# Layer 0 of a graph network: values split in two halves, second moments half a batch later in the order

## The chip, the cores and the metric

The kernel runs on one core of one Trainium2 chip. The metric is the device time of the whole program in microseconds (us). Engines are named TensorE (matmul; PE in the profile, with PEld for its weight loads), VectorE (DVE), ScalarE (ACT), GpSimd (POOL), and SyncE (SP), which issues loads.

## The reference

Sixteen graphs of 1024 nodes with 128 features go through four layers, each followed by a residual sum and a layer norm. Only layer 0 is touched here. Per graph, `adj` is a 0/1 matrix:

```python
w = masked_row_softmax(transpose(adj))      # row: region, column: node
region = matmul(w, features)
region = batch_norm(matmul(region, kernel_1) + bias_1, gamma_1, beta_1)
people = matmul(transpose(w), region)
people = batch_norm(matmul(people, kernel_2) + bias_2, gamma_2, beta_2)
x = layernorm(x + people)
```

Since the entries are 0 or 1, the softmax row is the mask divided by the number of its ones (the degree). Both batch norms take mean and variance over all graphs and nodes. Layers 1 to 3 are attention layers over the same graphs.

## The kernel before, in words

All arrays of a graph ("batch" b, 16 of them) are cut into C = 8 chunks of 128 rows. The kernel has two stages. The first, up to about 395 us, is class `Pass`: it reads `adj` once and computes for every batch mask-times-features, and then transposed-mask times that, without the small matrices. As batch norms are linear once their statistics are known, it gathers only the first and second moments of both results (`moments1`, `moments2`, each one PSUM bank that accumulates over all batches). Then a short serial part turns the moments into scales. The second stage (classes `Norm` and `Batch`) finishes layer 0 from the stored products `people` and runs layers 1 to 3.

One batch of the first stage has these steps:

- `load` (line 483) loads `x` and splits it into a high part in the matmul's short format (ScalarE, line 488) and a low remainder (VectorE, line 489), both in `x2`.
- `cast` (line 495), per chunk: load 512 KB of `adj` into `at`, and convert it into the mask `m`; even chunks on VectorE (line 501), odd ones on ScalarE (line 499). `at` has four buffers, `m` three.
- `forth` (line 503), per chunk: eight matmuls into `pz`; ScalarE copies the low half into `lo` (line 508), VectorE adds both into `z` (line 509). The mask's row sums, the degrees, come out as an extra column.
- `split` (line 511), once: reciprocal degrees `r` (lines 513 to 516), `reg` = `z` times `r` (line 520), `v` = `reg` times `r` (line 523), and `v` parted into a high part on ScalarE (line 525) and a low remainder on VectorE (line 526), both in `v2`. `reg` and `v` have one buffer each.
- `moment1` (line 531), per chunk: `reg` times itself into `moments1`, two matmuls in the profile.
- `back` (line 536), per chunk: eight matmuls of the mask with `v2` into `pb`; ScalarE copies the low half (line 543), VectorE adds (line 544) into `g`.
- `moment2` (line 546), per chunk: `g` times itself into `moments2`.
- `store` (line 551): one statistics instruction on `g` and the DMA of `g` to `people`. `g` has two buffers, `pz` and `pb` two PSUM banks each.

The order is written out with due times (lines 555 to 564). A step of batch b gets a time in units of batches; the per-chunk steps are spread over 0.9 of a unit; all are sorted and traced in that order. So in unit b the core runs `forth` of batch b beside `moment1`, `back` and `moment2` of batch b - 1, and casts of batch b + 1. The sorted order sets priorities: an instruction whose inputs or buffer aren't there yet (in the planner's own estimate) lets later ones past on its engine. On the chip each engine then follows its planned list.

Of the kernel before, what the change touches and what calls it, by code (L numbers as in the profile page):

```python
# [8 lines left out]
F32 = mybir.dt.float32  # L9
# [3 lines left out]
ALU = mybir.AluOpType  # L13
# [3 lines left out]
P = 128  # L17
# [10 lines left out]
F32R = mybir.dt.float32r  # L28
# [362 lines left out]
def fast_path(ctx, tc, x, adj, adjt, k1, k2, w1, vecs, b_w, b_a, out, bad):  # L391


    nc = tc.nc
    B, N, D = x.shape
    C = N // P
    H = N // 512
    G = C // 4
    A = D + 1
# [34 lines left out]
    degs = const.tile([P, B, C], F32, name="degs")  # L434
# [33 lines left out]
    with tc.tile_pool(name="z_load", bufs=4) as zl, tc.tile_pool(name="z_mask", bufs=3) as zm, \  # L468
# [8 lines left out]
        class Pass:  # L477
# [30 lines left out]
                nc.scalar.copy(self.lo[:, c, :], pz[:, D:D + A])  # L508
                nc.vector.tensor_tensor(self.z[:, c, :], pz[:, :D], self.lo[:, c, :D], ALU.add)  # L509

            def split(self):

                nc.vector.tensor_copy(degs[:, self.b, :], self.lo[:, :, D])
                r = zw.tile([P, C], F32, name="r")
                nc.vector.tensor_scalar(r, self.lo[:, :, D], 1.0, None, ALU.max)
                nc.vector.reciprocal(r, r)
                self.reg = zw.tile([P, C, A + 1], F32, name="reg", bufs=1)
                nc.gpsimd.memset(self.reg[:, :, D:], 1.0)
                by = r[:, :, None]
                nc.vector.tensor_tensor(self.reg[:, :, :D], self.z, by.to_broadcast([P, C, D]),  # L520
                                        ALU.mult)
                v = zw.tile([P, C, A], F32, name="v", bufs=1)
                nc.vector.tensor_tensor(v, self.reg[:, :, :A], by.to_broadcast([P, C, A]), ALU.mult)
                self.v2 = zw.tile([P, C, 2, A], F32R, name="v2")
                nc.scalar.copy(self.v2[:, :, 0, :], v)
                nc.vector.tensor_tensor(self.v2[:, :, 1, :], v, self.v2[:, :, 0, :].bitcast(F32),  # L526
                                        ALU.subtract)
                self.g = zw.tile([P, C, A + 1], F32, name="g")
                nc.gpsimd.memset(self.g[:, :, A:], 1.0)

            def moment1(self, c):
                nc.tensor.matmul(moments1[:, :A + 1], self.reg[:, c, :D], self.reg[:, c, :],  # L532
# [22 lines left out]
        order = []  # L555
        for b in range(B):
            s = Pass(b)
            for t, fs in ((b - 1, (s.load,)), (b + 0.95, (s.split,)), (b + 2.1, (s.store,))):
                order += [(t, f) for f in fs]
            for t, f in ((b - 0.95, s.cast), (b, s.forth), (b + 1, s.moment1), (b + 1.05, s.back),  # L560
                         (b + 1.2, s.moment2)):
                order += [(t + 0.9 * c / C, lambda f=f, c=c: f(c)) for c in range(C)]
        for _, f in sorted(order, key=lambda o: o[0]):
            f()
# [135 lines left out]
    with tc.tile_pool(name="r_load", bufs=3) as loads, tc.tile_pool(name="r_rows", bufs=2) as rows, \  # L700
# [220 lines left out]
        order = []  # L921
# [47 lines left out]
def kernel(tc, x, adj, adjt, k1, k2, w1, vecs, b_w, b_a, out):  # L969
    nc = tc.nc  # L970
    with tc.tile_pool(name="keep", bufs=1) as keep:
        bad = keep.tile([1, 1], I32, name="bad")
        fast_path(tc, x, adj, adjt, k1, k2, w1, vecs, b_w, b_a, out, bad)

        again = nc.values_load(bad[0:1, 0:1])
        with tc.If(again > 0):
            general_path(tc, x, adj, adjt, k1, k2, w1, vecs, b_w, b_a, out)
# [39 lines left out]
```

## Time and profile before

The time is 1988.63 us, the median of 3 runs (1984.18 to 1992.79). The profiled execution took 1994.7 us with a mean granted TensorE clock of 0.951.

| in the first stage | value |
|---|---|
| TensorE busy, whole span | 1742.4 us, 87% |
| VectorE busy, whole span | 1536.7 us, 77% |
| ScalarE busy, whole span | 997.1 us, 50% |
| line 506, `forth` matmuls | 1024 of 306 ns |
| line 539, `back` matmuls | 1024 of 295 ns |
| line 520 / 523 / 526, VectorE, 1024 to 1032 elements | 1.23 us each, 16 times |
| line 525, ScalarE, the high part of `v` | 1.06 us, 16 times |
| TensorE's wait at line 547 (`moment2`) for `g` | 25.6 us in 14 waits |
| TensorE's wait at line 539 (`back`) for the low part of `v` | 14.4 us in 14 waits |

How to read it: matmuls are pipelined, so a matmul's listed duration is longer than the distance to the next one (some 130 ns within a `forth` group); idle time between matmuls counts, not the sum of their durations. A wait is put down to the instruction that ended it last.

### The profile page before, as it was taken

How to read it: one execution, taken by the hardware profiler on the slowest of the kernel's cores; microseconds unless marked ns; L12 is line 12 of the kernel's file. 1: busy time of each engine (PE TensorE's matmuls, PEld its weight loads, DVE VectorE, ACT ScalarE, POOL GpSimd, SP SyncE). 2: the span in 40 equal slices, each digit the busy share in tenths (PEclk: the TensorE clock that was granted, in tenths of full speed). 3: DMA queues.
4: the chain of work that ended last, by engine and by line, in shares of the span. 5: the costliest groups of instructions: out<-in, count | busy, mean ns of one | idle time of the engine just before them, and what ended most of it. 6: DMA issues, size and time to landing. Idle time of an engine off the chain costs nothing.

```text
span 1994.7 us, 26348 instructions
## 1 busy us (share of the span) xinstructions
PE 1742.4 (87%) x9453; PEld 1260.5 (63%) x9453; DVE 1536.7 (77%) x3707; ACT 997.1 (50%) x1793; POOL 147.8 (7%) x252
## 2 busy tenths in 40 slices
PE   6988888957879999999999998998999999999895
PEld 6988888833545666656565655665665656565574
DVE  4554444467979789897989798989889898979765
ACT  4533334235455565545555556465565545555533
POOL 0000000001001010101000101101010101000100
PEclk9999899968999999999999999999999999999998
DMA  8866565143413232241404041323222240402000
GB/s 298 282 238 222 208 232 189 40 146 118 149 59 95 69 96 92 72 133 32 151 25 141 23 142 55 110 69 102 76 94 95 70 133 32 130 14 71 11 1 23
DMA packets 110958, 216.39 MB, mean 108 GB/s; under 512 B 7776, under 2 KB 63712, under 8 KB 110816
## 3 DMA queue, kind: packets, MB, share of 16 engines
q1 hardware_dynamic: 108512, 206.08, 31.6%
q10 hardware_dynamic: 2304, 8.52, 1.1%
q8 instruction: 76, 1.25, 0.3%
q14 instruction: 66, 0.54, 0.1%
HBM read 197.67 MB, written 16.91 MB: 108 GB/s over the span
## 4 chain that ended last, share of the span: by engine, by line
PE 42%; DVE 35%; ACT 8%; DMA 6%; POOL 4%; issue 4%; SPq 0%; DVEq 0%; ACTq 0%
PE pacc L876 17%; PE pbig L863 6%; DVE e L834 5%; PE pb L539 5%; PE po L844 5%; DVE e L837 5%; PE pz L506 5%; DMA at<-in_adj_dram 4%; ACT m L499 2%; DVE ln_st L718 2%; PE moments L547 1%; DVE e L831 1%; POOL rs_t L442 1%; PE pacc L753 1%; DVE hn L813 1%
## 5 line engine op out<-in xcount | busy, mean ns | idle before, releaser
L844 PE MATMUL po<-e,hn 128*128 128x512 f32 x512 | 251.8, 621 | 13.9 <-ACT hn L841 13.7
L823 ACT ACTIVATE pen<-adjt,minus_root 128x1024 fp8e5<-128x1024 int32 x128 | 146.5, 1148 | 74.9 <-DMA adjt<-in_adjt_dram 74.5
L844 PEld LDWEIGHTS po<-e,hn 128*128 128x128 f32 x512 | 94.6, 195 | 131.2 <-issue 82.0
L506 PE MATMUL pz<-x,m 128*128 128x258 f32 x1024 | 164.9, 306 | 4.6 <-ACT m L499 2.3
L539 PE MATMUL pb<-v,m 128*128 128x258 f32 x1024 | 151.2, 295 | 15.8 <-DVE v L526 14.4
L834 DVE SCALAR_TENSOR_TENSOR e<-u,q,u 128x1024 f32<-128x1024 f32 x128 | 161.4, 1271 | 0.3 <-ACT q L816 0.3
L837 DVE SCALAR_TENSOR_TENSOR e<-e,adjt 128x1024 f32<-128x1024 f32 x128 | 154.5, 1216 | 0.0
L539 PEld LDWEIGHTS pb<-v,m 128*128 128x128 f32 x1024 | 137.0, 198 | 18.7 <-DVE v L526 17.0
L506 PEld LDWEIGHTS pz<-x,m 128*128 128x128 f32 x1024 | 140.4, 202 | 7.3 <-ACT m L499 3.4
L880 DVE TENSOR_SCALAR sums<-pacc 128x3 f32<-128x3 f32 (+1 forms) x96 | 14.5, 151 | 145.9 <-PE pacc L876 145.9
L544 DVE TENSOR_TENSOR g<-pb,lo 128x129 f32<-128x129 f32 x128 | 36.4, 291 | 97.6 <-ACT lo L543 97.3
L841 ACT ACTIVATE hn<-hn,rs 128x128 f32<-128x128 f32 x128 | 49.9, 398 | 119.6 <-DVE rs L840 91.8
L831 DVE SCALAR_TENSOR_TENSOR e<-adjn,adjt 128x1024 f32<-128x1024 int32 (+7 forms) x128 | 95.2, 744 | 6.2 <-PE po L844 3.9
L499 ACT CAST m<-at 128x1024 fp32r<-128x1024 int32 x64 | 67.5, 1054 | 62.4 <-DMA at<-in_adj_dram 62.4
L509 DVE TENSOR_TENSOR z<-pz,lo 128x128 f32<-128x128 f32 x128 | 35.7, 288 | 76.4 <-ACT lo L508 76.2
L508 ACT COPY lo<-pz 128x129 f32<-128x129 f32 x128 | 34.1, 267 | 83.8 <-PE pz L506 83.0
L547 PE MATMUL moments<-g 128*128 128x130 f32 x256 | 53.1, 290 | 25.6 <-DVE g L544 25.6
L543 ACT COPY lo<-pb 128x129 f32<-128x129 f32 x128 | 33.0, 268 | 72.2 <-PE pb L539 72.1
L501 DVE CAST m<-at 128x1024 fp32r<-128x1024 int32 x64 | 43.8, 685 | 21.3 <-DMA at<-in_adj_dram 21.3
L547 PEld LDWEIGHTS moments<-g 128*128 128x128 f32 x256 | 41.6, 200 | 28.2 <-issue 27.2
L532 PE MATMUL moments<-reg 128*128 128x130 f32 x256 | 39.8, 279 | 2.8 <-DVE reg L520 2.1
L813 DVE TENSOR_TENSOR hn<-pacc,bw_row 128x387 f32<-128x387 f32 (+1 forms) x48 | 23.0, 502 | 21.3 <-PE pacc L811 21.0
(1169 smaller groups left out, 4239.1 us busy)
## 6 DMA issues: line engine op xcount, KB each, us to landing
at<-in_adj_dram SPq DMA_DIRECT2D x128, 512.0 KB, 5.3
adjt<-in_adjt_dram SPq DMA_DIRECT2D x128, 512.0 KB, 3.5
people<-g ACTq DMA_DIRECT2D x16, 520.0 KB, 5.9
g<-people SPq DMA_DIRECT2D x16, 520.0 KB, 4.6
xf<-in_x_dram SPq DMA_DIRECT2D x16, 512.0 KB, 6.3
adjn<-in_adj_dram SPq DMA_DIRECT2D x16, 512.0 KB, 4.4
x<-in_x_dram SPq DMA_DIRECT2D x16, 512.0 KB, 4.7
adjn<-in_adj_dram SPq DMA_DIRECT2D x16, 448.0 KB, 4.5
```

What stands on the lines that cost most here:

```text
L499: nc.scalar.copy(self.m[:, i, :], at)
L506: nc.tensor.matmul(pz[:, :2 * A], self.m[:, i, c * P:(c + 1) * P], self.x2[:, i, :], start=(i == 0), stop=(i == C - 1))
L539: nc.tensor.matmul(pz[:, :2 * A], self.m[:, j, c * P:(c + 1) * P], self.v2[:, j].rearrange("p s a -> p (s a)"), start=(j == 0), stop=(j == ...
L547: nc.tensor.matmul(moments2[:, :A + 1], self.g[:, c, :D], self.g[:, c, :], start=(self.b == 0 and c == 0), stop=(self.b == B - 1 and c == ...
L823: nc.scalar.activation(self.pen[:, c, :], at, AF.Square, bias=minus_root, scale=BIG_ROOT, saturate=False, accum_out=checks[:, self.b, c:c ...
L831: nc.vector.scalar_tensor_tensor(e[:, :n], an[:, :n], 1.0, at[:, c * P:], ALU.mult, ALU.not_equal, accum_out=unlike[:, self.b, c:c + 1])
L834: nc.vector.scalar_tensor_tensor(e, self.u2, self.q[:, c:c + 1], self.u1, ALU.mult, ALU.max)
L837: nc.vector.scalar_tensor_tensor(e, e, 1.0, at, ALU.mult, ALU.mult, accum_out=total)
L841: nc.scalar.mul(self.hn[:, c, :D], self.hn[:, c, :D], rs)
L844: nc.tensor.matmul(self.po[:, cols], self.hn[:, c, :D], e[:, cols], start=(c == 0), stop=(c == C - 1))
L863: nc.tensor.matmul(ps[:, cols], self.xw[:, c * P:(c + 1) * P], self.xt[:, cols], start=True, stop=True)
L876: nc.tensor.matmul(po[:, k, :], self.e[:, m, c * P:(c + 1) * P], xl[:, m, :], start=(m == 0), stop=(m == C - 1))
```

## The change

`split` becomes two calls, `split(0)` on chunks 0 to 3 and `split(1)` on chunks 4 to 7. The first also makes the tiles `reg`, `v2` and `g` and their constant columns. `r` and `v` are now half as large, and `v` has two buffers. The first half is due at b + 0.48, when half of `forth` has been traced, the second at b + 0.93 (the whole was at b + 0.95). In the order, `moment1` goes from b + 1 to b + 1.05, `back` from b + 1.05 to b + 1.12, `moment2` from b + 1.2 to b + 1.6, and `store` from b + 2.1 to b + 2.6. The purpose is that the values for `back` are prepared while `forth` is still running, and that the second moments aren't asked for right after the `back` that makes their `g`.

```diff
-            def split(self):
-                nc.vector.tensor_copy(degs[:, self.b, :], self.lo[:, :, D])
-                r = zw.tile([P, C], F32, name="r")
-                nc.vector.tensor_scalar(r, self.lo[:, :, D], 1.0, None, ALU.max)
+            def split(self, h):
+                if h == 0:
+                    self.reg = zw.tile([P, C, A + 1], F32, name="reg", bufs=1)
+                    nc.gpsimd.memset(self.reg[:, :, D:], 1.0)
+                    self.v2 = zw.tile([P, C, 2, A], F32R, name="v2")
+                    self.g = zw.tile([P, C, A + 1], F32, name="g")
+                    nc.gpsimd.memset(self.g[:, :, A:], 1.0)
+                n = C // 2
+                c = slice(h * n, (h + 1) * n)
+                nc.vector.tensor_copy(degs[:, self.b, c], self.lo[:, c, D])
+                r = zw.tile([P, n], F32, name="r")
+                nc.vector.tensor_scalar(r, self.lo[:, c, D], 1.0, None, ALU.max)
                 nc.vector.reciprocal(r, r)
...
-                nc.vector.tensor_tensor(self.reg[:, :, :D], self.z, by.to_broadcast([P, C, D]),
-                                        ALU.mult)
-                v = zw.tile([P, C, A], F32, name="v", bufs=1)
-                nc.vector.tensor_tensor(v, self.reg[:, :, :A], by.to_broadcast([P, C, A]), ALU.mult)
...
-                nc.scalar.copy(self.v2[:, :, 0, :], v)
-                nc.vector.tensor_tensor(self.v2[:, :, 1, :], v, self.v2[:, :, 0, :].bitcast(F32),
+                nc.vector.tensor_tensor(self.reg[:, c, :D], self.z[:, c, :],
+                                        by.to_broadcast([P, n, D]), ALU.mult)
+                v = zw.tile([P, n, A], F32, name="v", bufs=2)
+                nc.vector.tensor_tensor(v, self.reg[:, c, :A], by.to_broadcast([P, n, A]), ALU.mult)
+                nc.scalar.copy(self.v2[:, c, 0, :], v)
+                nc.vector.tensor_tensor(self.v2[:, c, 1, :], v, self.v2[:, c, 0, :].bitcast(F32),
                                         ALU.subtract)
...
-            for t, fs in ((b - 1, (s.load,)), (b + 0.95, (s.split,)), (b + 2.1, (s.store,))):
-                order += [(t, f) for f in fs]
-            for t, f in ((b - 0.95, s.cast), (b, s.forth), (b + 1, s.moment1), (b + 1.05, s.back),
-                         (b + 1.2, s.moment2)):
+            order += [(b - 1, s.load), (b + 0.48, lambda s=s: s.split(0)),
+                      (b + 0.93, lambda s=s: s.split(1)), (b + 2.6, s.store)]
+            for t, f in ((b - 0.95, s.cast), (b, s.forth), (b + 1.05, s.moment1),
+                         (b + 1.12, s.back), (b + 1.6, s.moment2)):
                 order += [(t + 0.9 * c / C, lambda f=f, c=c: f(c)) for c in range(C)]
```

More of the change, by code (lines that the diff above doesn't have):

```diff
@@ L516, in split @@
                 nc.vector.reciprocal(r, r)
-                self.reg = zw.tile([P, C, A + 1], F32, name="reg", bufs=1)
-                nc.gpsimd.memset(self.reg[:, :, D:], 1.0)
                 by = r[:, :, None]
-                nc.vector.tensor_tensor(self.reg[:, :, :D], self.z, by.to_broadcast([P, C, D]),
-                                        ALU.mult)
-                v = zw.tile([P, C, A], F32, name="v", bufs=1)
-                nc.vector.tensor_tensor(v, self.reg[:, :, :A], by.to_broadcast([P, C, A]), ALU.mult)
@@ L524, in split @@
-                self.v2 = zw.tile([P, C, 2, A], F32R, name="v2")
-                nc.scalar.copy(self.v2[:, :, 0, :], v)
-                nc.vector.tensor_tensor(self.v2[:, :, 1, :], v, self.v2[:, :, 0, :].bitcast(F32),
+                nc.vector.tensor_tensor(self.reg[:, c, :D], self.z[:, c, :],
+                                        by.to_broadcast([P, n, D]), ALU.mult)
+                v = zw.tile([P, n, A], F32, name="v", bufs=2)
+                nc.vector.tensor_tensor(v, self.reg[:, c, :A], by.to_broadcast([P, n, A]), ALU.mult)
@@ L527, in split @@
+                nc.scalar.copy(self.v2[:, c, 0, :], v)
+                nc.vector.tensor_tensor(self.v2[:, c, 1, :], v, self.v2[:, c, 0, :].bitcast(F32),
                                         ALU.subtract)
-                self.g = zw.tile([P, C, A + 1], F32, name="g")
-                nc.gpsimd.memset(self.g[:, :, A:], 1.0)
             def moment1(self, c):
```

## The prediction

> **What bounds the kernel now.** I read the page first. Layer 0 (`Pass`, lines 477 to 564) is the first fifth of the span, up to about 395 us, and the diff touches nothing after it. I then cut that stage into stretches of 5 us, TensorE alone.
>
> ```profile
> core 0: us, PE busy (x), PEclk, DMA share, GB/s
> ...
> 240.00:245.00 5.00, 4.94 (x42) 1.00 0.36 114
> 245.00:250.00 5.00, 2.34 (x18) 1.00 1.06 394
> 250.00:255.00 5.00, 4.77 (x27) 0.66 1.02 386
> 255.00:260.00 5.00, 5.00 (x44) 1.00 0.50 165
> 260.00:265.00 5.00, 5.00 (x44) 1.00 0.00 0
> ```
>
> A batch has a good part (44 matmuls in 5 us, no DMA) and a bad part: 18 matmuls in one stretch, because TensorE is idle, then 27 in the next, because its clock is granted at 0.66. The pattern recurs in nearly every batch. The copy of line 513, once per batch, gives the period: from 93.96 to 360.15 us there are 11 periods, 24.2 us each. The last one, from 360.15 to 379.42, has no loads left and takes 19.3 us. So about 4.9 us per batch are lost, some 54 us over those 11. Next, who makes TensorE wait (from 20 to 392 us).
>
> ```profile
> PE moments L547 <- DVE g L544: 25.3, 13, 3.1
> PE pb L539 <- DVE v L526: 14.4, 14, 1.1
> PE moments L532 <- DVE reg L520: 2.1, 2, 1.3
> ```
>
> Two waits, each once per batch: second moments for `g` (1.95 us each time), `back` for the low half of the values `v2` (1.03 us). The order of time in one batch says why.
>
> ```profile
> 242.46 1.06 ACT L525 CAST v<-v 128x1032 fp32r<-128x1032 f32 x1 [0.18 <-DVE v L523]
> 242.54 1.22 DVE L489 TENSOR_TENSOR x<-xf,x 128x1024 fp32r<-128x1024 f32 x1
> ...
> 243.67 0.69 DVE L501 CAST m<-at 128x1024 fp32r<-128x1024 int32 x1
> ...
> 243.88 1.28 PE L532 MATMUL moments<-reg 128*128 128x130 f32 x10
> ...
> 244.36 0.68 DVE L501 CAST m<-at 128x1024 fp32r<-128x1024 int32 x1
> ...
> 244.95 1.23 DVE L526 TENSOR_TENSOR v<-v,v 128x1032 fp32r<-128x1032 f32 x1
> ...
> 246.23 2.19 PE L539 MATMUL pb<-v,m 128*128 128x258 f32 x16 [1.08 <-DVE v L526]
> ...
> 248.54 1.04 ACT L499 CAST m<-at 128x1024 fp32r<-128x1024 int32 x1 [4.20 <-DMA at<-in_adj_dram]
> 249.49 0.43 ACT L543 COPY lo<-pb 128x129 f32<-128x129 f32 x2
> 249.79 0.49 DVE L544 TENSOR_TENSOR g<-pb,lo 128x129 f32<-128x129 f32 x2 [2.61 <-ACT lo L543]
> ...
> 250.23 0.46 PE L547 MATMUL moments<-g 128*128 128x130 f32 x2 [1.81 <-DVE g L544]
> ```
>
> Each row: start and length in us, engine, line, operation, and in brackets the idle time before it and its releaser. First stall: the split is one serial chain over all 8 chunks, ScalarE's copy of `v` leaves VectorE with nothing of the split to do, and the x subtraction and two casts (1.22 + 0.69 + 0.68) go in ahead of the last subtraction. TensorE spends its fillers (five first moments in one burst) and still stands for 1.08 us. Second stall: on ScalarE a cast waits 4.20 us for its DMA, and the copy `lo` of two finished `back` groups is behind it. `g` is late, and the second moment is next in TensorE's queue. Then the clock drops.
>
> **What the skill says.** "TensorE: Matmul & The Clock Gate", Part 1 (the HAM clock gate): the clock falls to half after an idle window of about 3.4 us and comes back after a busy one. The trace agrees on level and length: the record has eight spells at 0.5 between 93 and 360 us, seven of 3.41 us and one of 6.83. It differs on the trigger: here 1.08 and 1.81 us of idleness, two matmul groups between them, were enough. Same page, "Architectural detail": ScalarE and VectorE take instructions strictly in order. The `lo` copy behind the waiting cast agrees. "VectorE: DVE Perf Modes", the section on the TRN2 errata: each instruction pays a fixed cost, so halves cost more than a whole. Line 513 (8 elements) takes 0.162 us, line 520 (1024) 1.226 us, which agrees.
>
> **The change, part by part.**
>
> *Splitting.* Three VectorE operations of about 1.23 us become two halves each, and the three small ones (0.162, 0.166, 0.203) are doubled. Half size isn't in the trace: the low end is half of 1.226, 0.61 us; a line through `z` (128 elements, 0.288) and `reg` (1024, 1.226) gives 0.288 + 384 x 1.047 ns = 0.69 us. I take 0.69. Extra on VectorE: 3 x (2 x 0.69 - 1.23) + 0.53 = 1.0 us per batch (low end 0.5). ScalarE's copy of 1.061 us, by its own line through `lo` (129, 0.268), becomes 2 x 0.61: 0.16 us more. Over 16 batches 16 and 2.5 us of engine time. In layer 0 VectorE is busy 11 to 12 us of each 23 and ScalarE 9, so I cost both at nothing: TensorE's 19.3 us per batch hide them.
>
> *The chain.* From the last `z` (239.14 + 0.29 = 239.43) to the end of line 526 (246.18) it is 6.75 us now. Afterwards only the second half follows the last `forth`: small ones about 0.45, `reg` 0.69, `v` 0.69, copy 0.61, subtraction 0.69, together 3.1 us. The first half isn't free to run at b + 0.48, though: `reg` has one buffer, and `moment1` of the batch before reads it until b + 0.8375. The chain of waits already shows this dependency (GpSimd's memset of `reg` behind line 532, 86.7 us in all). So the first half comes late too, and puts up to 3 x 0.69 = 2.1 us in front: 3.1 to 5.2 us. But its steps fill VectorE while ScalarE copies, where casts slip in now, and `back` starts on chunks 0 to 3 when only the first half is done. Cover: before the first `back` TensorE has the old batch's last `back`, two `forth` groups (each about 1.05 us) and a few moments of 0.23 us: 3.7 us, and 1.6 us more of first moments to pull ahead. That meets the chain. Removed: 14.4 us, and perhaps 1 to 2 more in the last batch, where nothing else overlaps.
>
> *Second moments at +1.6.* Each moves from one group after its `back` to four groups after; the number of matmuls stays. TensorE no longer asks for a `g` just being made, and has four leftovers of the older batch as fillers at each batch start. What stays is the cast waiting for its DMA on ScalarE, with `lo` behind it. `pb` and `pz` have two PSUM buffers each, so TensorE can run two groups of each kind, about 4 us, before it needs that copy. The longest cast wait is 5.5 us, the usual one 4.2. So the wait mostly fits in, not wholly: I take two thirds of 25.3 us as removed, 17 us (ends: 0, if the wait moves to the next `back`, and all 25).
>
> *Clock.* Seven spells of 3.41 us and one of 6.83, at half speed, cost 30.7 / 2 = 15 us of full-clock work. With the first stall gone and the second shortened I take half to two thirds away: 8 us (ends 0 and 15).
>
> *Rest.* The store at +2.6 needs only a finished `g`, and can be issued as early as now if ScalarE's queue is free. Its two buffers suffice: the next writer comes at b + 1.12 of two batches later. The memsets only move. Zero.
>
> Sum: 14 + 17 + 8 = 39 us, 1988.6 - 39 = 1950 us.
>
> **The rivals.**
>
> *The wait changes its name* (chance 0.20). `back` 2 waits for the PSUM buffer that `lo` and `g` must free, as long as `moment2` waited for `g`. For it: the DMA burst stays, about 400 GB/s for 10 us, and ScalarE's cast still stands in its way. Against: two buffers of each kind are about 4 us. Then only the `v` wait goes: 1989 - 14 = 1975 us.
>
> *Nearly everything goes* (0.20). All idleness and the slow spells: 14.4 + 25.3 + 15 = 55 us, 1934 us. For it: the batch without loads runs at 19.3 us with the same code. Against: that batch has no casts at all.
>
> *Slower* (0.12). The first half is held by the single `reg` buffer and both halves run one after the other with their extra 1.0 us; a cast waiting on VectorE gets between them, and late `v2` holds `back`. For it: casts do wait on VectorE (about 1 us per batch on line 501), and the first moments that hold `reg` are placed 0.05 of a batch later than before. One to two us more per batch for 14 batches, on top of the present stalls: about 2005 us. Against: less of the chain is left after the last `forth` than now in any case.
>
> **How the numbers follow.** Forecast 0.48, rivals 0.20, 0.20, 0.12. Predicted is the likeliest, 1950 us. The range goes from 1925 (everything gone, and a few us of noise) to 1983 (the wait renamed, with less gained than the 14 us); outside are the slow case and small tails. Faster by over 0.5% (under 1978.7): the forecast, everything, and a bit over half of the renamed wait, 0.78. Within 0.5%: 0.11. Slower: 0.11.
>
> **What would show it.** Right: TensorE's wait for `v` at line 539's place near zero; its wait for `g` under 10 us in total; a period under 22 us; fewer slow-clock spells before 360 us; VectorE's busy time up by about 16 us. Wrong: TensorE's `back` or `forth` waiting for ScalarE or VectorE once per batch for 2 us (renamed wait), a wait of `reg` or of first moments on the first half (slower), or a change of the time after layer 0, which no step here expects.

## The result, and the profile after

The changed kernel takes 1962.66 us, the median of 4 runs (1955.41 to 1969.08), against 1986.71 us in the same comparison. The ratio is 0.9873, with a 95% interval of 0.9831 to 0.9916. Timed again with the experiments it gave 1960.19 us, ratio 0.9855 (0.9835 to 0.9875). So 24 to 28 us are gone where 39 were forecast.

All of it lies in the first stage. Its last second moment starts at 395.2 us before and at 370.0 after, 25.2 us earlier; what follows takes 1599.5 us before (1994.7 - 395.2) and 1597.1 after (1967.1 - 370.0).

TensorE's waits in the first stage after the change (what waited, for whom: us in total, times, longest), to compare with the three lines in the prediction:

```profile
PE pb L543 <- DVE g L548: 23.8, 11, 2.6
...
PE pz L506 <- ACT m L499: 1.9, 3, 1.3
...
PE pz L506 <- DVE z L509: 0.9, 2, 0.5
...
PE pb L543 <- DVE v L532: 0.3, 1, 0.3
```

The wait for `v` is gone (14.4 to 0.3 us), and so is the one for `reg` (2.1). The wait for `g` is nearly all there (25.3 to 23.8), but another instruction does the waiting: `back` (line 543) instead of the second moments. A second profile of the same kernel (experiment 5) has 20.0 us for `g`, again in 11 waits, and 2.2 for `v`; single profiles of one kernel differ by that much. The batches follow each other in 22.6 us (87.61 to 336.15, 11 periods) instead of 24.2. The order of time in one batch shows the wait.

```profile
161.64 1.08 PE L543 MATMUL pb<-v,m 128*128 128x258 f32 x7
...
164.00 1.14 PE L543 MATMUL pb<-v,m 128*128 128x258 f32 x8
...
165.72 0.60 PE L506 MATMUL pz<-x,m 128*128 128x258 f32 x3
167.19 1.04 ACT L499 CAST m<-at 128x1024 fp32r<-128x1024 int32 x1 [3.21 <-DMA at<-in_adj_dram]
168.14 0.43 ACT L547 COPY lo<-pb 128x129 f32<-128x129 f32 x2
...
168.44 0.49 DVE L548 TENSOR_TENSOR g<-pb,lo 128x129 f32<-128x129 f32 x2 [2.71 <-ACT lo L547]
...
168.78 1.79 PE L543 MATMUL pb<-v,m 128*128 128x258 f32 x8 [2.46 <-DVE g L548]
```

Two `back` groups are done by about 165 us and fill both PSUM banks of `pb`. ScalarE has stood since 163.98 before a cast whose load lands at 167.19; the copies of both groups (x2) come only after it, so the third `back` has no bank. TensorE stands for 2.46 us, and then its clock drops: the matmuls that follow take 1.79 us for eight, where 1.14 is usual. The Trainium skill's page "Perfetto Trace Analysis", section "Identifying Performance Opportunities", says that the same gap repeating on the engine that should be saturated can mean too few SBUF or PSUM buffers for the next tile. That fits here: a third bank for `pb` (experiment 3) takes most of the gap away.

Spells at half clock before the stage's end, from the clock record: 8 with 30.7 us before, 7 with 23.9 us after (6 with 20.5 in the second profile). The sum of what changed: 14.1 (`v`) + 2.1 (`reg`) + 1.5 (`g`) + (30.7 - 23.9) / 2 = 3.4 for the clock, 21 of 25 us; the rest is not put down to one cause. The second profile gives 12.2 + 2.1 + 5.3 + 5.1, 25 of 29 us.

### The profile page after: what moved, and what is told of

Its sections match the earlier page's. It is cut to its first block, busy times and chain, and to the rows that moved or that the text cites. A ratio compares the mean times of both kernels' runs of the same rounds, so it can differ in the third digit from the quotient of the medians.

```text
span 1967.1 us, 26476 instructions
## 1 busy us (share of the span) xinstructions
PE 1735.1 (88%) x9453; PEld 1258.0 (64%) x9453; DVE 1540.6 (78%) x3803; ACT 997.4 (51%) x1809; POOL 148.1 (8%) x252
## 4 chain that ended last, share of the span: by engine, by line
PE 41%; DVE 35%; ACT 8%; DMA 7%; issue 4%; POOL 4%; SPq 0%; DVEq 0%; ACTq 0%
PE pacc L880 17%; PE pbig L867 6%; DVE e L838 5%; PE po L848 5%; DMA at<-in_adj_dram 5%; PE pb L543 5%; DVE e L841 5%; PE pz L506 3%; DVE ln_st L722 1%; DVE e L835 1%; ACT m L499 1%; POOL rs_t L442 1%; PE pacc L757 1%; DVE hn L817 1%; PE moments L536 1%
## 5 line engine op out<-in xcount | busy, mean ns | idle before, releaser
L543 PE MATMUL pb<-v,m 128*128 128x258 f32 x1024 | 156.8, 295 | 24.2 <-DVE g L548 23.8
L536 PE MATMUL moments<-reg 128*128 128x130 f32 x256 | 48.9, 279 | 0.1
L551 PE MATMUL moments<-g 128*128 128x130 f32 x256 | 48.4, 274 | 0.0
L536 PEld LDWEIGHTS moments<-reg 128*128 128x128 f32 x256 | 39.0, 194 | 0.4 <-issue 0.3
```

Source lines behind the costliest of these rows:

```text
L543: nc.tensor.matmul(pz[:, :2 * A], self.m[:, j, c * P:(c + 1) * P], self.v2[:, j].rearrange("p s a -> p (s a)"), start=(j == 0), stop=(j == ...
```

## The experiments

Ratios are to the kernel before, with 95% intervals. In the diffs, "before" or "changed" is said for the kernel that was edited.

**1. Halves alone** (changed kernel, old due times):

```diff
-                      (b + 0.93, lambda s=s: s.split(1)), (b + 2.6, s.store)]
+                      (b + 0.95, lambda s=s: s.split(1)), (b + 2.1, s.store)]
-            for t, f in ((b - 0.95, s.cast), (b, s.forth), (b + 1.05, s.moment1),
-                         (b + 1.12, s.back), (b + 1.6, s.moment2)):
+            for t, f in ((b - 0.95, s.cast), (b, s.forth), (b + 1, s.moment1),
+                         (b + 1.05, s.back), (b + 1.2, s.moment2)):
```

> The split in halves at b + 0.48 and b + 0.95, with the old due times of moment1, back, moment2 and store. Theory (the halves took the wait for v away, the later second moments only renamed the wait for g): TensorE's wait for v under 2 us in all instead of 14.4, its wait for g stays about 25 us at moment2, time about 1970 us. Rival (the new due times brought the gain): v is still waited for, about 1987 us.

Measured: 1953.17 us, 0.9846 (0.9817 to 0.9875). The theory's first half holds: TensorE's wait for `v` is 0.5 us. Its wait for `g`, at the second moments, fell to 12.4 us and the slow spells to 10.2 us, without any move of the second moments; the theory had it at 25. Why it fell is open. The halves alone give as much as the whole change.

**2. Due times alone** (before, split whole at b + 0.93, `moment1` at 1.05, `back` at 1.12, `moment2` at 1.6, `store` at 2.6):

> The new due times of moment1, back, moment2 and store, with the split whole at b + 0.93. Theory: back still waits for v, some 10 to 14 us in all, and for g through the PSUM buffers, some 20 us; about 1980 us. Rival (the later second moments are the useful part): waits for v nearly gone because leftover moments fill the gap, about 1965 us.

Measured: 1958.17 us, 0.9861 (0.9837 to 0.9886). The rival's figures came: the wait for `v` is 3.5 us. Its reason, the later second moments by themselves, does not hold (experiment 9). The order of time around one split shows what stands in the gap: second moments of the older batch (line 547) among the first moments (line 532), until `back` starts without a wait.

```profile
178.95 1.20 PE L506 MATMUL pz<-x,m 128*128 128x258 f32 x8
179.99 0.38 PE L547 MATMUL moments<-g 128*128 128x130 f32 x2
180.21 0.39 PE L532 MATMUL moments<-reg 128*128 128x130 f32 x2
180.43 0.39 PE L547 MATMUL moments<-g 128*128 128x130 f32 x2
180.66 0.39 PE L532 MATMUL moments<-reg 128*128 128x130 f32 x2
180.88 0.39 PE L547 MATMUL moments<-g 128*128 128x130 f32 x2
181.10 1.06 PE L532 MATMUL moments<-reg 128*128 128x130 f32 x8
182.29 1.21 PE L539 MATMUL pb<-v,m 128*128 128x258 f32 x8
```

The wait for `g` through PSUM is 11.2 us, slow spells 10.2 us. So either part alone gives the gain of both; the three intervals overlap, and their gains don't add.

**5. The changed kernel again**, on one chip with runs 6 to 8:

> The changed kernel itself again, so that the parts and the whole are compared on one chip. Both theories: about 1962 us, ratio 0.987 to before; if either part alone is really better than both together, it is slower than the 1953 us of the halves alone.

1960.19 us, 0.9855 (0.9835 to 0.9875): slower than the halves alone by 7 us in the median, but those were timed on another chip, and the intervals of the ratios overlap; which is better stays open.

**9. Second moments alone** (before, with `moment2` at 1.6 and `store` at 2.6; all else at its old time):

> The kernel before with only the second moments (b + 1.6) and the store (b + 2.6) moved; split whole at b + 0.95, moment1 and back at their old times. Theory (left-over second moments are what fills the gap before the first back): wait for v under 5 us, wait for g at back's PSUM bank about 11 us, time as with all new due times, 1953 to 1963 us. Rival (the later back is what fills it): wait for v stays near 14 us, about 1980 us.

1978.33 us, 0.9959 (0.9943 to 0.9974). The theory fell. The rival had the time, but its wait for `v` was too small. TensorE's waits:

```profile
PE pb L539 <- DVE v L526: 27.2, 13, 3.4
...
PE pb L539 <- DVE g L544: 0.5, 1, 0.5
```

The wait for `g` is gone and the wait for `v` has doubled. In one batch VectorE had a cast in front of line 526 that waited 1.43 us for its load, and `back` stood for 2.19 us. The later second moments, without the other due times, mostly choose which of the two waits is paid: together they are 27.7 us instead of 39.7, and the slow spells stay at 30.7 us. The leftover second moments are there in this run too, so they alone don't cover the wait for `v`. What in the other due times (split at 0.93, `moment1`, `back`) makes experiment 2 so much better was not separated.

**3. A third PSUM bank for `pb`** (changed kernel):

```diff
-            tc.tile_pool(name="z_back", bufs=2, space=PSUM) as zb, \
-            tc.tile_pool(name="z_tr", bufs=2, space=PSUM) as zt, \
+            tc.tile_pool(name="z_back", bufs=3, space=PSUM) as zb, \
+            tc.tile_pool(name="z_tr", bufs=1, space=PSUM) as zt, \
```

> The changed kernel with three PSUM banks for pb instead of two (taken from the bank pair of the short serial part after the stage). Theory (the renamed wait is for the PSUM bank of pb): TensorE can run one more back group of 1.05 us before it stands, so 23.8 us of waits shrink by about 11 x 1.05 to some 12 us, and fewer slow-clock spells; about 1950 us. Rival (the cast on ScalarE holds pz as well, so that the wait goes on to forth): no gain, 1960 to 1966 us.

1938.81 us, 0.977 (0.9747 to 0.9792), better than the theory's 1950. The wait shrank by more than one group each time, and no spell at half clock is left in the stage:

```profile
PE pb L543 <- DVE g L548: 6.6, 9, 1.1
```

**6. The third bank in the kernel before:**

> The kernel before with three PSUM banks for pb. Theory (before, the second moment stands in TensorE's queue right behind the back group and waits for g itself, so a further bank for back can't be reached): wait for g at moment2 stays 20 to 25 us, time 1980 to 1990 us. Rival (the banks alone were the limit, in either order): below 1965 us.

1988.47 us, 1.0003 (0.9988 to 1.0017). The wait for `g` at the second moments stays:

```profile
PE moments L547 <- DVE g L544: 24.5, 13, 2.9
```

As forecast: the bank is of no use while an instruction ahead of the next `back` waits for the same copy. The profile of this run has five slow spells with 17.1 us, where the kernel before has eight with 30.7, at the same waits and the same median time. So the spells of a single profile vary by that much.

**7. Halves with the third bank, old due times:**

> Split in halves, old due times, three PSUM banks for pb. Theory (the bank pays only where second moments are asked for late): the remaining 12 us of waits for g at moment2 stay, time about 1950 us, at least 8 us slower than new due times with three banks (1939 us). Rival (the later second moments are of no use once the values come in halves): 1935 to 1940 us.

1952.57 us, 0.982 (0.9796 to 0.9844), no gain over experiment 1. 16.6 us of waits for `g` at the second moments are left. So the third bank is reachable only with the new due times (experiment 3). That it is the second moments among them follows from where TensorE waits: here at the second moments, with the new due times at `back`.

**10. Due times with the third bank, split whole:**

> New due times, split whole at b + 0.93, three PSUM banks for pb. Theory (with the later second moments and a third bank the halves add nothing): 1935 to 1943 us, as halves with due times and three banks. Rival (the whole split makes TensorE wait for v again once it runs without the other stalls): wait for v back at 8 us or more, 1950 us or more.

1941.06 us, 0.9774 (0.9757 to 0.979), the same as experiment 3. With late second moments and three banks the halves add nothing that can be measured.

**4. The odd casts on GpSimd** (changed kernel):

```diff
                 if i % 2:
-                    nc.scalar.copy(self.m[:, i, :], at)
+                    nc.gpsimd.tensor_copy(self.m[:, i, :], at)
```

> The changed kernel with the odd casts of adj on GpSimd instead of ScalarE; nothing else moves, the same values are computed. Theory (the copy lo stands on ScalarE behind a cast that waits for its DMA): with no cast on ScalarE the wait for g falls from 23.8 to under 6 us, slow-clock spells before 360 us mostly go, about 1935 us, unless a GpSimd cast takes so long that forth waits for m. Rival (the DMA burst itself limits, by VectorE's casts too): the wait for g stays above 15 us, about 1960 us.

1944.83 us, 0.9791 (0.9769 to 0.9814). The wait for `g` is down to 0.2 us, though the casts wait for their loads longer than on ScalarE (116.9 us instead of 44.0), and there is no slow spell. So the burst of loads harms through the queue that its cast stands in; that ScalarE is also spared the casts themselves (1.05 us each) was not separated from this. The time is 10 us over the theory's, and the wait for `v` is back with 15.8 us. A likely cause is in the trace: of the 64 halves of `reg` and `v` on VectorE, 26 take 1.32 to 1.53 us instead of 0.68. Each of these began while a cast ran on GpSimd, and none of the other 38 did. One lasts from 94.30 to 95.62 us, beside a cast that ends at 95.08.

**8. Five load buffers for `adj`** (changed kernel, `bufs=4` to `bufs=5` in `z_load`; in the serial part the two `_rep`, the two `_outer` and the two `quad` tiles share one buffer each, to make room):

> The changed kernel with five load buffers for adj instead of four (room made by sharing three small tiles in the serial part). Theory (ScalarE's cast waits for a load that could only be issued when a buffer came free): one more chunk is there ahead of time, ScalarE's waits for the load fall from 44 us by at least a third, TensorE's wait for g from 23.8 to about 10 us, about 1950 us. Rival (the burst is limited by the DMA rate alone): waits and time as in the changed kernel, 1960 to 1966 us.

1951.3 us, 0.9809 (0.9786 to 0.9832). The time is the theory's, its mechanism isn't: ScalarE's waits for loads stay at 43.3 us and TensorE's for `g` at 18.4. What fell is the slow clock, two spells with 6.8 us. Only two of its eleven waits put 1.8 us or more into one step of the clock record; the last section says why that counts. The sharing was not run by itself. It touches only what comes after the stage, and that takes 1591 to 1600 us in every profile here, with the sharing (1593.8, in experiments 11 and 12 1599.3 and 1592.1) and without.

**11. Two buffers for `reg`** (changed kernel, room made as in 8):

```diff
-                    self.reg = zw.tile([P, C, A + 1], F32, name="reg", bufs=1)
+                    self.reg = zw.tile([P, C, A + 1], F32, name="reg", bufs=2)
```

> The changed kernel with two buffers for reg instead of one (room made by sharing three small tiles in the serial part), so that the first half may run while moment1 still reads the older reg. Theory (the wait for v is gone already, the single buffer costs nothing): wait for g stays 18 to 25 us, 1955 to 1965 us. Rival (the first half, held back until the batch's end, crowds VectorE where the casts come): wait for g down to 12 us or less, 1950 us.

1936.51 us, 0.974 (0.9721 to 0.9759). The theory fell: the time is 18 us under its lower end. The wait for `g` is down to 2.6 us in 3 waits, and no slow spell is left. With the second buffer the two halves of `reg` are made half a batch apart; first here, then in the changed kernel, where both come at the batch's end:

```profile
156.39 0.69 DVE L527 TENSOR_TENSOR reg<-z,r 128x512 f32<-128x512 f32 x1
...
165.73 0.69 DVE L527 TENSOR_TENSOR reg<-z,r 128x512 f32<-128x512 f32 x1
```

```profile
158.00 0.68 DVE L527 TENSOR_TENSOR reg<-z,r 128x512 f32<-128x512 f32 x1
...
159.61 0.68 DVE L527 TENSOR_TENSOR reg<-z,r 128x512 f32<-128x512 f32 x1
```

What the buffer is worth is measured; how it comes about is read from one batch and was not tested by itself. TensorE then alternates between `forth` and `back` from a batch's start, one moment of each kind in between, and keeps its pace through the burst of loads. A batch takes 19.4 us (87.42 to 300.72, 11 periods), about as long as the one without loads in the kernel before (19.3). Stretches of one batch, TensorE alone (length, busy and count of matmuls, clock, share and GB/s of the DMA):

```profile
150.00:155.00 5.00, 5.00 (x44) 1.00 0.81 259
155.00:160.00 5.00, 5.00 (x43) 1.00 1.02 412
160.00:165.00 5.00, 5.00 (x44) 1.00 0.89 305
165.00:170.00 5.00, 5.00 (x44) 1.00 0.24 88
```

**12. The third bank and five load buffers together** (room made as in 8):

> The changed kernel with three PSUM banks for pb and five load buffers for adj. Theory (both cut the same stall, and three banks alone leave 6.6 us of it and no slow clock): 1933 to 1940 us, no more than 5 us under three banks alone. Rival (the load buffers take away a stall of their own): below 1931 us.

1929.58 us, 0.9713 (0.9697 to 0.9729), the fastest kernel here: 57 us under the kernel before. It is 9 us under the bank alone, so the theory's 5 us are passed and the rival's time came. Its wait for `g` is 1.4 us, and the stage's last second moment starts at 330.4 us. Two buffers for `reg` together with three banks were not run.

## Why the prediction was right, and where it was not

*The wait for `v`: right.* 14.4 us were to go and 14.1 went (12.2 in the second profile). But the halves weren't needed for it: experiment 2 removes most of it with the split whole. The cover that the other due times give was not counted. The leftover second moments, named as fillers in the prediction's next paragraph, are part of it, but not enough (experiment 9).

*The wait for `g`: wrong, and the largest miss.* The step took 17 of 25.3 us as removed, because two PSUM buffers of each kind were "about 4 us" of reserve against a usual cast wait of 4.2. The trace after shows 1.5 us removed, the second profile 5.3. The reserve is not full when the cast begins to block: ScalarE stands from 163.98 us with one `back` group finished and its copy still ahead, and TensorE runs dry about 166.3, after 2.3 us and not 4. The rival "the wait changes its name" described this mechanism and was given 0.20; its time, 1975, was 12 us too high, of which the wait for `reg` and the clock, both left out, are some 5. The prediction's own sign of this came true: `back` waits for VectorE about once per batch for 2 us. Experiments 3, 6 and 10 confirm the bank, and experiment 4 the cast on ScalarE.

*The clock: mis-sized.* 8 us were forecast; the profiles show 6.8 to 10.2 us of spells less, worth 3 to 5 us. That is within what single profiles vary by (experiment 6), so even the direction is not shown. The prediction hung the spells on both stalls. The eight spells before follow the wait for `g` alone (last section), and that wait stayed. Where it is nearly gone (3, 4, 11, 12) no spell is left.

*The single buffer of `reg`: seen, and costed wrongly.* The prediction said that the first half would be held until the older `moment1` is done, and then asked only whether `v` would still be in time. It was in time, but the purpose of the early half was lost: both halves and the casts crowd the batch's end, where the trace has VectorE without a pause. Experiment 11 puts the price at 24 us, as much as the whole change gained. In the "slower" rival the same fact was used for a longer `v` chain, which never came.

*Splitting: right.* A half of `reg` takes 0.685 us (0.69 taken). By durations this is 1 us more per batch; VectorE's busy time rose by only 2.1 us in 11 batches (129.73 to 131.87), not the 1 us in each, since neighbouring durations overlap. The work is hidden as forecast.

*The rest: right.* What follows the stage changed by 2.4 us, less than it varies from profile to profile (1591 to 1600 us).

The sum was 14 + 17 + 8 = 39; measured it is 14 + 1.5 + 3.4, with 2.1 for `reg` that was left out and about 4 not assigned. That the time lies in the range is luck as far as the mechanism goes: the range was wide enough to hold the renamed wait as well, and the largest term of the sum did not come.

## What to carry to other kernels

When an instruction that waits is moved away, look up what stands next in its queue and whether that needs the same producer by way of a buffer: here the move was worth 28 us (experiment 2), the buffer alone nothing (experiment 6), both together 46 (experiment 10). Before work is split to start earlier, check that its output has a buffer to start into; one buffer of `reg` held back what the halves were for. And a load that arrives late costs most when its cast stands in the queue of the engine that empties PSUM: with the casts elsewhere they waited 116.9 us, and TensorE 0.2 us for `g`. But the engine that takes the casts can hold up another (experiment 4).

## What the runs showed of the hardware

A single stall of about 2.5 us (166.3 to 168.78) was enough for a spell of 3.41 us at half clock, and in the kernel before 1.81 us. The Trainium skill's page "TensorE: Matmul & The Clock Gate", Part 1, gives an idle window of about 3.4 us as the trigger; the measurement decides here.

Whether a stall triggers depends on where it falls. In each trace with spells, their starts in the stage lie whole multiples of 3.41 us apart (in the changed kernel 100.91, 124.80, 169.17 and so on: 7, then 13 steps), so the clock record has fixed steps. Here are the steps around three stalls, with the fields as above: in the kernel before a wait for `v` and one for `g`, in the changed kernel a wait of 2.40 us for `g` (236.39 to 238.78) that falls across the border of two steps.

```profile
244.37:247.78 3.41, 2.33 (x20) 1.00 0.98 381
247.78:251.20 3.42, 1.61 (x14) 1.00 1.12 401
251.20:254.61 3.41, 3.41 (x18) 0.50 1.00 375
```

```profile
234.03:237.44 3.41, 2.36 (x20) 1.00 0.99 404
237.44:240.85 3.41, 2.07 (x17) 1.00 1.03 420
240.85:244.27 3.42, 3.42 (x32) 1.00 0.92 304
```

The 1.08 us of idleness for `v` have a step of their own and trigger nothing; the 1.81 us in the next one do. So the two stalls that the prediction added up do not add. The 2.40 us, parted by the border into 1.05 and 1.34, trigger nothing either. Over all traces, 44 spells of the stage begin after its first 40 us, and TensorE was idle for 1.79 to 3.07 us in the step ahead of each. Of the other 858 steps at full clock in these traces only five have 1.79 us or more, at most 1.88. Two spells in the first 40 us follow less (0.97 and 0.98 us). The idle times rest on modelled ends of matmuls, so the bound, about 1.8 us of a step, is an estimate. In experiment 8 two of eleven waits reach it within a step (2.66 and 1.90 us), the others stay under 1.7.

GpSimd and VectorE can hold each other up: in experiment 4 half of `reg` or `v` that began while a GpSimd cast ran took 1.32 us or more instead of 0.68, and eleven casts that began within 0.07 us after such a half took 1.52 to 1.58, where the shortest take 1.04.

On VectorE an instruction of half the size costs about half in a dense row: the half `v` starts at 158.81 us and its successor at 159.41, 0.60 us apart, with a listed duration of 0.68; the whole was 1.14 us apart (241.20 to 242.34), with 1.22 listed. By the starts of this pair, two halves cost 0.06 us more than the whole; by durations it is 0.14. More than half of the fixed cost is overlapped by the next instruction.
